# Four small edits around the turn between two images: where sums steps, a row copy, a table load and spilled rows are placed

## The chip, the cores and the metric

The kernel runs on one core of one Trainium2 chip. The metric is the time of one execution on the device in microseconds (us), lower is better. The runs of one kernel mostly lie within 0.2 to 0.5% of each other (no_logs: 1.0%), so a single difference below some 8 us means little; the tables give the medians of several runs and ratios with 95% intervals. All runs told here were in the fast state.

PE is TensorE's matrix array, PEld its weight load, DVE VectorE, ACT ScalarE, POOL GpSimd and SPq the queue from which SyncE starts DMA transfers. L333 means line 333 of that kernel's source; line numbers shift by a few between kernels.

## The reference, cut to what matters

Eight images of 256 channels and 96 x 96 pixels pass through two layers with residuals.

```python
# x: (8, 256, 96, 96) float32
x = x + L0(group_norm(x))   # q, k, v = three 1x1 convolutions, each fft2; q, k normalised;
                            # attention of 32 x 32 per head over frequencies; abs(ifft2); 1x1 convolution
x = x + L1(group_norm(x))   # q = softplus(Wq x + bq), k = softplus(Wk x + bk), v = Wv x + bv;
                            # linear attention: (q . k v) / (q . sum k)
```

## The kernel before

The kernel works through the images in turn. Five stages matter here. The *sums* of an image are 37 steps, each with four transposes (`eoT`), one copy by ScalarE, two sums (`eo`) by VectorE or GpSimd and eight product passes (`acc`). They belong to the next image and are woven as fillers between the matmuls of the present one: `yield n` in a stage lets n of those steps run. The *rotation* transposes all rows of an image (`xr`) and multiplies them by a table (`y`). Then come the *images* stage, the *q and k* stage with the key transposes (`kT`) behind it, and the *output* stage (`o`), whose stores write the image out. The *turn* is the time from the output stage's first matmul to the next image's first `xr` transpose; sums steps that are left over run in it.

```python
T0 = 6                                     # tiles T0 .. 11 of an image go by DRAM, already transposed

def pair_sums(b):                          # one step
    ...
    nc.scalar.activation(both, pt, AF.Copy, scale=pw[:, j:j + 1])
    if b and t >= T0:
        n = P - j // 2                     # 128 or 127 partitions
        for c in range(2):
            nc.sync.dma_start(out=turned(c, PR * t, 1 + P * j)[0:n], in_=both[0:n, c])
    ...
    pool = (j if t < T0 else t > NT - 4) if b and i < len(steps) - 5 else None   # which sums GpSimd takes
    ...
    yield

def rotate(b):
    ...
    o = x_col(0)                           # row 0 into the half that the last image is stored from
    nc.gpsimd.tensor_copy(y[:, :, :, 0], x_of(b)[:, :, o:o + W])
    nc.gpsimd.memset(ys[:, :, 0:1], 0.0)
    ...
    pieces = [TR * i for i in (15, 4, 0, 5, 14, 6, 1, 8, 13, 7, 2, 9, 12, 10, 3, 11)]

def layer1(b):
    for s in range(NS):
        ...                                # two q and k matmul groups, DVE relu, ACT Abs and Exp
        yield 0.5
    ...
    yield 2
    ...                                    # softplus: ACT table load and Ln, DVE adds; then kT
```

Of the kernel before, what the change touches and what calls it, by code (L numbers as in the profile page):

```python
# [53 lines left out]
AF = mybir.ActivationFunctionType  # L54
# [6 lines left out]
D = 32  # L61
ROWS = 8
TR = 6
T0 = 6
NZ = 33
NH = 8
GN_EPS = 1e-5
# [5 lines left out]
def two_layer_kernel(ctx: ExitStack, tc: tile.TileContext, x, w1t, b1, w2t, b2, w3, b3, wot, temp,  # L73
# [26 lines left out]
    def x_of(b):  # L100
        return arenas[b % 2]
# [218 lines left out]
        return t.rearrange("p k (h w) -> p k h w", w=W)  # L320

    s0 = {}

    def pair_sums(b):

        st0 = new_stats(f"st0_{b}")
        acc = [acc_tile(f"acc{c}_{b}") for c in range(2)]

        def products(t, np_, first, last):
            for c in range(2):  # L330
                for m in range(KC):
                    mm = nc.tensor.matmul(acc[c][:, m * C:m * C + (KC - m) * P], lhsT=t[0:np_, c, m * P:(m + 1) * P],  # L332
                                          rhs=t[0:np_, c, m * P:C], start=(first and m == 0), stop=(last and c == 1),  # L333
                                          skip_group_check=True)
                    if first and m:
                        tc.keep_in_program_order(mm)

        x = x_of(b)

        w0 = one.tile([P, KC, H + 1], F32, tag="ys", name=f"w0_{b}")  # L340
        nc.gpsimd.memset(w0[:, :, H // 2:H // 2 + 1 + PR * T0], 0.0)

        def sides(t, j):

            o = (NT - 1 - t) * TW + (t == 0) * W + 1 + P * j
            e = (NT - t) * TW - (t == 0) * W - 1 - P * j
            if t or j < 2:
                return [(0, P, x[:, :, o:o + P], x[:, :, e:e - P:-1])]
            m = H // 2
            rows = [x[:, :, x_col(h):x_col(h) + W] for h in (0, H // 2)] + [w0]  # L350
            if j == 2:
                return [(0, 32, x[:, :, o:o + 32], x[:, :, e:e - 32:-1])] + [
                    (32 * i + 32, 32, v[:, :, 1:33], v[:, :, W - 1:W - 33:-1] if i < 2 else w0[:, :, m + 2:m + 34])
                    for i, v in enumerate(rows)]

            return [(32 * i, 32, v[:, :, m:m + 32], v[:, :, m:m - 32:-1]) for i, v in enumerate(rows[0:2])] + [
                (64, 32, w0[:, :, 32:64], None), (64, 16, None, w0[:, :, m + 33:m + 49]), (80, 16, None, w0[:, :, m:m + 16]),
                (96, 32, rows[0][:, :, 0:32], rows[0][:, :, 0:32])]

        back = three.tile([P, TR * (W + 1)], F32, tag="tm", name=f"back_{b}")[:, 0:2 * C].rearrange(  # L360
            "p (i k n) -> p i k n", i=2, k=KC)

        def turn_back(i):

            t, j = steps[i]
            assert (b, t) in loaded
            if j == 0:
                col = x[:, :, (NT - 1 - t) * TW:(NT - t) * TW:W]
                h, o = PR * t, H // 2 + 1 + PR * t
                nc.gpsimd.tensor_copy(w0[:, :, h:h + PR], col[:, :, 0:PR])  # L370
                if t:
                    nc.gpsimd.tensor_copy(w0[:, :, o:o + PR], col[:, :, :PR - 1:-1])
                else:
                    nc.gpsimd.tensor_copy(w0[:, :, o:o + 1], col[:, :, 0:1])
                    nc.gpsimd.tensor_copy(w0[:, :, o + 1:o + PR], col[:, :, 2 * PR - 2:PR - 1:-1])
                    nc.gpsimd.tensor_copy(w0[:, :, o - 1:o], col[:, :, 2 * PR - 1:])
            if j == 0:
                xts.append(ring_tile(f"xt_{b}_{t}_{j}").rearrange("p (j c n) -> p j c n", j=3, c=2))
            ab = sides(t, j)
            ready = len(ab) == 1  # L380

            front = ab[0][2] if ready else xts[-1][:, j % 3, 0].rearrange("p (k n) -> p k n", k=KC)
            for p0, n, *v in ab:
                for c in range(ready, 2):
                    if v[c] is not None:
                        (nc.scalar.copy if b and t < T0 and (ready or not c) else nc.gpsimd.tensor_copy)(
                            (front, back[:, i % 2])[c][:, :, p0:p0 + n], v[c])
            return front, xts[-1][:, j % 3]

        steps = [(t, j) for t in range(NT - 1, -1, -1) for j in range(3)] + [(0, 3)]  # L390
        pending, first = None, True
        xts = []
        ahead = turn_back(0)
        for i, (t, j) in enumerate(steps):
            front, both = ahead
            pt = ps_tile(f"eoT_{b}_{t}_{j}").rearrange("p (c n) -> p c n", c=2)
            for k in range(KC):
                nc.tensor.transpose(pt[:, 0, k * P:(k + 1) * P], front[:, k], ident)
                nc.tensor.transpose(pt[:, 1, k * P:(k + 1) * P], back[:, i % 2, k], ident)  # L399
            nc.scalar.activation(both, pt, AF.Copy, scale=pw[:, j:j + 1])  # L400
            if b and t >= T0:
                n = P - j // 2
                for c in range(2):
                    nc.sync.dma_start(out=turned(c, PR * t, 1 + P * j)[0:n], in_=both[0:n, c])
            eo = sum_slot()[:, :, 0:C]
            if i + 1 < len(steps):
                ahead = turn_back(i + 1)

            pool = (j if t < T0 else t > NT - 4) if b and i < len(steps) - 5 else None
            for c, (op, on_pool) in enumerate(((ALU.add, nc.gpsimd.tensor_add), (ALU.subtract, nc.gpsimd.tensor_sub))):  # L410
                if pool or pool is None and c:
                    on_pool(eo[:, c], both[:, 0], both[:, 1])  # L412
                else:
                    nc.vector.scalar_tensor_tensor(eo[:, c], in0=pt[:, 0], scalar=pw[:, j:j + 1], in1=both[:, 1],  # L414
                                                   op0=ALU.mult, op1=op)
            if pending is not None:
                products(*pending, first, False)
                first = False
            pending = (eo, P)
            if j in (1, 2):  # L420
                stats_chunk(st0, b, 2 * (NT - 1 - t) + j - 1)
            if (t, j) == (0, 1):
                wl = ring_tile(f"wl_{b}").rearrange("p (k o) -> p k o", k=KC)
                for o, v in enumerate((w1t, w2t, w3)):
                    nc.sync.dma_start(out=wl[:, :, o * C:(o + 1) * C], in_=v.rearrange("(k p) o -> p k o", p=P))
            if b and (t, j) == (T0, 2):
                n = H // 2 - PR * T0
                pt = ps_tile(f"w0T_{b}")
                col = xts[-2][:, 0, 0]
                for k in range(KC):  # L430
                    nc.tensor.transpose(pt[0:H + 1 - PR * T0, k * P:(k + 1) * P], w0[:, k, PR * T0:H + 1], ident)
                nc.scalar.copy(col[0:H + 1 - PR * T0], pt[0:H + 1 - PR * T0, 0:C])
                for c in range(2):
                    o = c * (H // 2 + 1)
                    nc.sync.dma_start(out=xtd[c].rearrange("(h w) n -> h w n", w=W)[:, 0], in_=col[o:o + n])
            yield
        s0[b] = channels(st0, f"a{b}"), acc, products, pending, wl
# [158 lines left out]
    def rotate(b):  # L596

        y = image(y_of(b))
        ys = one.tile([P, KC, H + 1], F32, tag="ys", name=f"ys_{b}")
        o = x_col(0)  # L600
        nc.gpsimd.tensor_copy(y[:, :, :, 0], x_of(b)[:, :, o:o + W])
        nc.gpsimd.memset(ys[:, :, 0:1], 0.0)

        def spilled(h):

            return b > 0 and PR * T0 <= h < H - PR * T0 and h != H // 2
# [18 lines left out]
            return tm  # L625


        pieces = [TR * i for i in (15, 4, 0, 5, 14, 6, 1, 8, 13, 7, 2, 9, 12, 10, 3, 11)]
        order = [h + r for h in pieces for r in range(0, TR, 2)]
        xts = {}  # L630

# [38 lines left out]
        for i, h in enumerate(order):  # L670
            if i % (TR // 2) == 0:
                tm = tms.pop(0)
            if i % (TR // 2) == 2 and i > 2 and pieces:
                tms.append(load_r(pieces.pop(0)))
            if not spilled(h):
                xts[i] = xT[:, i % NX]
            step(None if spilled(h) else h, pending.pop(0) if len(pending) == 2 else None, xts[i])
            pending.append((h, xts.pop(i), tm))
            fetch(i + 3)
            yield  # L680
# [110 lines left out]
    def layer1(b):  # L791
# [30 lines left out]
        for s in range(NS):  # L822
            n = slice(s * CH, (s + 1) * CH)
            for c in range(2):
# [7 lines left out]
                                        op0=ALU.add, op1=ALU.max)  # L832
                nc.scalar.activation(ex[:, c, n], ps[:, 0:CH], AF.Abs, bias=bkqs[:, c:c + 1])
                nc.scalar.activation(ex[:, c, n], ex[:, c, n], AF.Exp, scale=-1.0)
            yield 0.5
        zero = own[:, 5 * C:5 * C + 1]
        nc.scalar.activation(zero, ex[:, 1, NS * CH - 1:NS * CH], AF.Copy, scale=0.0)

# [6 lines left out]
            nc.tensor.matmul(pv[:, 0:C], lhsT=nmb[:, k, :], rhs=wvs[:, k, :], start=(k == 0), stop=(k == KC - 1))  # L845
        nc.vector.tensor_add(bvs, bvs, pv[:, 0:C])

        yield 2

        def softplus(c, s):  # L850

# [228 lines left out]
```

## Time and profile before

| quantity | value |
|---|---|
| time, median of 4 runs | 2750.23 us (2745.97 to 2752.4); 2748.91 in the three known at the prediction |
| PE busy in the profiled run | 2682.8 us, 98% |
| turn, seven images | 48.5 to 51.0 us, mean 49.6 |
| q and k stage, to the first `kT` | 26.6 us, of it PE idle 1.57 |
| rotation, to the images stage | 65.6 us |
| spells at half clock, between 60 and 2600 us | three of 3.4 us |

PE is nearly always busy, so only its work and its few waits count. The prediction below shows and reads the lines: the wait for GpSimd's sum at the turn, where the row copy stands in front of that sum and itself waits for the stores, and the wait for ScalarE behind the logarithms. The rows from the turn down come from the starts of the instructions in the trace and from its records of the clock; "clock" is the granted TensorE clock.

### The profile page before, as it was taken

To read this page: it belongs to the slowest core of one execution; us is meant where nothing else is said; L and a number is where in the kernel's file an instruction comes from. 1 tells how busy PE (TensorE), PEld (TensorE's weight loads), DVE (VectorE), ACT (ScalarE), POOL (GpSimd) and SP (SyncE) were. 2 spreads that over 40 slices of the span, in tenths; PEclk is the share of its full clock that TensorE was granted. 3 is DMA by queue.
4 is the path that set the end of the run, shared out by engine and by line. 5 is a ranking of instruction groups with operands and counts; after the bars stand their busy time and mean duration, and the time that the engine had idled before them with its cause. 6 is when DMAs were issued, how large, how long until landed. Compare 5 with 4: busy or idle time off the path is not lost. (4 is left out here: it accounts for less than half of the span.)

```text
span 2744.9 us, 47959 instructions
## 1 busy us (share of the span) xinstructions
PE 2682.8 (98%) x17718; PEld 1934.5 (70%) x17718; DVE 1971.2 (72%) x4246; ACT 1363.4 (50%) x2167; POOL 854.3 (31%) x1284
## 2 busy tenths in 40 slices
PE   8999999999999999999999999999999999999988
PEld 8965678657795677856678567785677856778556
DVE  6678666886668766687676876769767686677766
ACT  3455643556425564255642546435564355644554
POOL 6133340333404424044140441413414134141311
PEclk9999999999999999999999999999999999999997
DMA  5220264202542026320263203631036311262003
GB/s 174 70 68 12 70 219 129 74 10 96 204 110 69 15 93 207 101 69 20 95 208 103 58 26 99 207 101 52 28 99 210 102 46 33 96 217 70 1 7 138
DMA packets 216407, 261.38 MB, mean 95 GB/s; under 512 B 32624, under 2 KB 204272, under 8 KB 216176
## 3 DMA queue, kind: packets, MB, share of 16 engines
q1 hardware_dynamic: 215232, 257.99, 30.1%
q8 instruction: 142, 2.33, 0.4%
q14 instruction: 89, 0.73, 0.1%
q10 hardware_dynamic: 944, 0.34, 0.0%
HBM read 145.75 MB, written 112.51 MB: 94 GB/s over the span
## 5 line engine op out<-in xcount | busy, mean ns | idle before, releaser
L732 PE MATMUL z<-arena,mz 128*128 128x384 f32 (+2 forms) x2400 | 595.0, 476 | 0.0
L744 PE MATMUL po<-e,wo 128*128 128x384 f32 x1536 | 529.7, 486 | 0.2 <-ACT e L779 0.2
L778 POOL TENSOR_TENSOR e<-e 128x768 f32<-128x768 f32 x192 | 348.7, 1816 | 552.0 <-ACT e L777 551.7
L732 PEld LDWEIGHTS z<-arena,mz 128*128 128x128 f32 (+1 forms) x2400 | 325.6, 163 | 241.4 <-issue 42.4
L332 PE MATMUL acc<-xT 128*128 128x256 f32 (+1 forms) x2368 | 451.7, 332 | 28.2 <-POOL xT L412 16.7
L332 PEld LDWEIGHTS acc<-xT 128*128 128x128 f32 x2368 | 385.0, 192 | 72.5 <-POOL xT L412 19.1
L744 PEld LDWEIGHTS po<-e,wo 128*128 128x128 f32 x1536 | 289.4, 190 | 197.7 <-DVE arena L746 1.2
L656 PE MATMUL y<-tm,xT 96*128 96x97 f32 x3040 | 424.1, 268 | 3.6 <-ACT xT L665 2.9
L773 DVE TENSOR_TENSOR e<-z,xT 128x768 f32<-128x768 f32 x384 | 365.8, 953 | 84.9 <-PE z L732 84.8
L656 PEld LDWEIGHTS y<-tm,xT 96*128 96x128 f32 x3040 | 411.9, 192 | 16.5 <-issue 7.4
L286 DVE BATCH_NORM_STATS2 st<-arena 128x6 f32<-128x384 f32 x768 | 409.4, 553 | 13.3 <-DMA arena<-in_x_dram 2.9
L779 ACT ACTIVATE e<-e 128x768 f32<-128x768 f32 x192 | 162.0, 844 | 337.9 <-POOL e L778 336.9
L777 ACT ACTIVATE e<-e 128x1536 f32<-128x1536 f32 x192 | 284.5, 1482 | 90.3 <-DVE e L773 88.8
L400 ACT ACTIVATE xt<-eoT,pw 128x512 f32<-128x512 f32 x296 | 202.9, 688 | 194.7 <-PE eoT L399 180.3
L746 DVE TENSOR_TENSOR arena<-arena,po 128x384 f32<-128x384 f32 x384 | 211.3, 552 | 90.5 <-PE po L744 67.7
L412 POOL TENSOR_TENSOR xT<-xt 128x256 f32<-128x256 f32 x324 | 236.0, 745 | 63.6 <-ACT xt L400 62.9
L665 ACT COPY xT<-xr 96x512 f32<-96x512 f32 (+1 forms) x223 | 127.5, 576 | 249.1 <-PE xr L653 249.1
L653 PE MATMUL xr<-ident,arena 128*96 128x128 f32 x876 | 229.3, 275 | 0.0
L662 DVE COPY arena<-y 128x384 f32<-128x384 f32 (+1 forms) x384 | 208.9, 547 | 1.8 <-issue 1.2
L414 DVE SCALAR_TENSOR_TENSOR xT<-eoT,pw,xt 128x256 f32<-128x256 f32 x268 | 119.4, 478 | 125.2 <-ACT xt L400 124.9
L661 DVE COPY ys<-y 128x4 f32<-128x4 f32 (+1 forms) x384 | 61.9, 161 | 151.8 <-PE y L656 149.0
L981 DVE TENSOR_TENSOR arena<-arena,o 128x384 f32<-128x384 f32 x288 | 142.6, 550 | 37.3 <-PE o L976 37.2
(227 smaller groups left out, 3254.3 us busy)
## 6 DMA issues: line engine op xcount, KB each, us to landing
arena<-in_x_dram SPq DMA_DIRECT2D x184, 384.0 KB
out_dram<-arena SPq DMA_DIRECT2D x184, 384.0 KB
xT<-xtd SPq DMA_DIRECT2D x161, 192.0 KB
tm<-rx SPq DMA_DIRECT2D x108, 218.2 KB
xtd<-xt SPq DMA_DIRECT2D x168, 128.0 KB
xtd<-xt SPq DMA_DIRECT2D x84, 127.0 KB
rx<-tm SPq DMA_DIRECT2D x16, 218.2 KB
tm<-rt SPq DMA_DIRECT2D x16, 216.0 KB
```

What stands on the lines that cost most here:

```text
L286: nc.vector.bn_stats(out=st[:, k, c, :], in_=x_of(b)[:, k, c * CH:(c + 1) * CH])
L332: mm = nc.tensor.matmul(acc[c][:, m * C:m * C + (KC - m) * P], lhsT=t[0:np_, c, m * P:(m + 1) * P], rhs=t[0:np_, c, m * P:C], start=(first ...
L412: on_pool(eo[:, c], both[:, 0], both[:, 1])
L653: nc.tensor.transpose(pt[0:W, r * C + k * P:r * C + (k + 1) * P], x_of(b)[:, k, o:o + W], ident)
L656: nc.tensor.matmul(pu[:, o:o + W + 1], lhsT=gt[0:W, 1 - r if back else r, k * P:(k + 1) * P], rhs=tm[:, g % TR + r, :], start=True, stop=True)
L662: nc.vector.tensor_copy(y[:, :, :, g + r:g + 2], src[:, :, 0:W, r:2] if back else src[:, :, W - 1::-1, r:2])
L732: mm = nc.tensor.matmul(out[:, o:o + n * W], lhsT=columns(mz, k, c, j), rhs=y[:, k, h * W:(h + n) * W], start=(k == 0 and o == 0), stop=(k ...
L744: nc.tensor.matmul(po[:, 0:CH], lhsT=wo[:, k, m * P:(m + 1) * P], rhs=e[:, k, :], start=(k == 0), stop=(k == KC - 1))
L746: nc.vector.tensor_add(x[:, m, n], x[:, m, n], po[:, 0:CH])
L773: nc.vector.tensor_add(e[:, 2 * c:2 * c + 2, :].rearrange("p t (q h) -> p t q h", h=H), pz[:, 0:CH].rearrange("p (q h) -> p q h", h=H).uns ...
L777: nc.scalar.activation(e, e, AF.Square)
L778: nc.gpsimd.tensor_add(e[:, 0:2, :], e[:, 0:2, :], e[:, 2:4, :])
```

## The change

Its intent: spill a seventh tile by DRAM, so that 16 transposes an image go; issue row 0's copy with its rows instead of ahead of the rotation; let whole instead of half sums steps run beside q and k, so that fewer are left at the turn; and hold the logarithms back until one step's copy is out. The rule for which sums GpSimd takes (`i < 13`) was changed with the seventh tile. It was not run alone; what bounds its worth is said further below.

```diff
-T0 = 6
+T0 = 5
+    evicted = {}
...
+            evicted[0] = both
...
-            pool = (j if t < T0 else t > NT - 4) if b and i < len(steps) - 5 else None
+            pool = (j if t < T0 else i < 13) if b and i < len(steps) - 5 else None
...
-        o = x_col(0)
-        nc.gpsimd.tensor_copy(y[:, :, :, 0], x_of(b)[:, :, o:o + W])
-        nc.gpsimd.memset(ys[:, :, 0:1], 0.0)
...
-        pieces = [TR * i for i in (15, 4, 0, 5, 14, 6, 1, 8, 13, 7, 2, 9, 12, 10, 3, 11)]
+        pieces = [TR * i for i in (15, 4, 0, 5, 6, 14, 8, 3, 1, 7, 9, 13, 10, 12, 11, 2)]
...
+            if h == 0:
+                o = x_col(0)
+                nc.gpsimd.tensor_copy(y[:, :, :, 0], x_of(b)[:, :, o:o + W])
+                nc.gpsimd.memset(ys[:, :, 0:1], 0.0)
...
-            yield 0.5
+            yield 1
...
-        yield 2
+        yield 1
+        if b + 1 < B:
+            nc.scalar.activation(zero, evicted[0][:, 0, 0:1], AF.Identity, scale=0.0, bias=zero)
+        yield 1
```

## The prediction

> **What bounds the kernel now.** I read the page, then the timeline of one image, engine by engine, then sums over stretches. The page says that PE is the bound:
>
> ```profile
> span 2744.9 us, 47959 instructions
> PE 2682.8 (98%) x17718; PEld 1934.5 (70%) x17718; DVE 1971.2 (72%) x4246; ACT 1363.4 (50%) x2167; POOL 854.3 (31%) x1284
> ```
>
> So a gain is either PE work taken away or one of the few PE waits. The list of PE's waits has two lines that come back with the images:
>
> ```profile
> PE acc L332 <- POOL xT L412: 16.7, 15, 2.8
> PE acc L332 <- DVE xT L414: 11.2, 8, 1.6
> ```
>
> The timeline shows where they sit. Images 1 to 7 repeat one pattern of about 336 us; I use image 1. The first is at the end of the sums (the turn into the next image), where PE has only sums left:
>
> ```profile
> 410.84 1.47 PE L332 MATMUL acc<-xT 128*128 128x256 f32 x8
> 412.58 0.82 PE L332 MATMUL acc<-xT 128*128 128x256 f32 x4
> 415.29 0.92 PE L332 MATMUL acc<-xT 128*128 128x256 f32 x4 [1.88 <-POOL xT L412]
> 421.46 1.04 PE L653 MATMUL xr<-ident,arena 128*96 128x128 f32 x8
> ...
> 414.12 0.52 POOL L601 COPY arena<-arena 128x192 f32<-128x192 f32 x1 [3.33 <-DMA wl<-in_w1t_dram]
> 414.50 0.73 POOL L412 TENSOR_TENSOR xT<-xt 128x256 f32<-128x256 f32 x1
> ```
>
> L601 is row 0's copy into the arena from which the previous image is still being stored. GpSimd is in order, so it stands 3.33 us before it, the sum L412 stands behind it, and PE waits for the sum. The releaser's name (a weight load) is a guess of the profile: the data that the copy must wait for are the stores. These are a bound of their own:
>
> ```profile
> 369.00:377.00 8.00, 8.00 (x52) 5.39 (x50) 5.82 (x13) 2.54 (x6) 1.72 (x3) 1.00 0.08 27
> 382.20:414.10 31.90, 31.20 (x224) 23.69 (x224) 25.00 (x54) 16.87 (x38) 20.95 (x38) 1.00 1.05 363
> ```
>
> The last two columns are DMA share and GB/s: from 382.2 to the very moment of the copy, 414.1, all DMA engines are full. The output stage's first matmul is at 372.8, so the stores are through 41.3 us after it, whatever PE does.
>
> The second wait is behind the logarithms, when q and k are done:
>
> ```profile
> 318.37 1.28 ACT L857 ACT_TABLE_LOAD   x1
> 319.66 1.12 ACT L857 ACTIVATE spu<-spu,own 128x384 f32<-128x384 f32 x2
> 320.69 1.24 ACT L400 ACTIVATE xt<-eoT,pw 128x512 f32<-128x512 f32 x2
> ...
> 322.29 1.57 PE L332 MATMUL acc<-xT 128*128 128x256 f32 x8 [1.57 <-DVE xT L414]
> ```
>
> ScalarE takes the table and two logarithms first; the step's copy (L400), transposed by 318.9, starts 1.8 us late.
>
> **What the Trainium skill says.** "ScalarE: Activation LUTs", section What ACT_TABLE_LOAD costs, gives about 1283 ns for a load; the trace has 1.28 us here, and five loads an image. "DMA: Bandwidth & Descriptors", section Why a DMA increments its semaphore by 16 and not by 1, says that a transfer of 127 partitions uses one DMA engine. The share of 0.08 from 369 to 377, with the 127-row writes just issued, agrees (one of 16 is 0.06). "TensorE: Matmul & The Clock Gate", section The HAM clock gate, says that PE drops to half rate after an idle window of about 3.4 us. The trace agrees in kind, not in length: after a wait of 2.8 us in image 5's turn the same transposes took
>
> ```profile
> 1763.13 0.42 PE L398 MATMUL eoT<-ident,xt 128*128 128x128 f32 x1
> ```
>
> against 0.27 us in image 1. "Perfetto Trace Analysis", section Identifying the Most-Contended Engine, warns that busy PE is no measure of headroom; so I count PE by starts of following instructions, not by its durations.
>
> **The change part by part.** Unit costs from starts in the timeline: a whole sums step (4 transposes, 8 product passes) is 1.74 us of PE (406.71 to 408.45, again to about 410.2). An image transpose is 0.11 us (8 between 421.46 and 422.34).
>
> *Seven tiles by DRAM.* The orders of both programs differ by 112 image transposes (876 to 764), 16 in each of seven images: 16 x 0.11 = 1.76 us an image, 12.3 in all, off PE. ScalarE loses 28 copies and 21 of its turned-back copies (these go to GpSimd); neither is the bound. DMA gains 28 reads of 192 KB and 42 writes. In the rotation VectorE then has less cover: a row pair costs it 0.16 + 0.55 us (L661, L662) against PE's 0.85 without transposes. From 432 to 437 it is busy 4.89 of 5.00 us now, and the new order of pieces puts six spilled pairs in a row. I leave 0.4 us an image for that: net -1.4.
>
> *Whole steps beside q and k.* Six steps instead of three there, three fewer at the turn. PE is full in both places, so this moves 3 x 1.74 = 5.2 us, and does not save it. The stage from 297.1 to the first kT at 323.7 grows by 5.2.
>
> *Logarithms behind a step's copy.* The 1.57 us wait goes. But the logarithms now start one copy later (two steps stand between the last kq and kT). From durations: the last kq's Abs and Exp, the copy, the load and one logarithm end about 6.0 us after the last kq, VectorE's add 0.55 later, and kT could start at 6.1. That is a new wait of 0 to 0.6; I take 0.3. Stage: +5.2 - 1.57 + 0.3 = +3.9.
>
> *Row 0's copy later.* In the new order of GpSimd the copy has moved behind all sums but one: the last step's second sum is still after it. So the turn does not become free of the stores. PE's three remaining steps would end early: the last transposes about 38.5 us after the output stage's first matmul, the previous products and the first half of the last about 40.5. Then PE waits for the copy at 41.3 (+0.39 to the next start), the sum 0.73, and the last four passes 0.65: image transposes start at about 43.2. Before it was 421.46 - 372.8 = 48.7. The turn gets 5.4 us shorter; of that, 5.2 is the steps that moved. PE's wait there stays about 2 us (before 1.88 in image 1), so cold clocks stay about as likely.
>
> Sum per image: turn -5.4, q and k +3.9, rotation -1.4, so -2.9; seven turns: -20 us. Image 0's own rotation changes only in order. 2748.9 - 20 = 2729.
>
> **Rivals.** (1) *The stores bind nothing, all waits go.* Then each image gains 1.76 + 1.57 + about 2 to 3 at the turn (the wait, its latency and the cold spells), some 6 us: 2748.9 - 42 = 2707. For it: copy and sums were meant to be untangled. Against it: one sum stays behind the copy in GpSimd's order, and the DMA row is at 1.05 until 414.1. (2) *DMA becomes the bound.* Two more 127-row writes an image on one engine, ahead of the stores in the same queue, could start the stores later; with a longer wait PE goes cold, 1.3 us more (image 5: 8.7 us from copy to first image transpose against 7.3). Reads of 192 KB a pair every 0.85 us, with the row tables, ask some 300 GB/s in the runs of spilled pairs. That could cost 2 to 3 us an image: about 2748, the same. For it: the full DMA row. Against it: tile 5 is written at the same place before the output stage as tile 6 was, because the sums run three steps earlier, and the rotation now moves 124 GB/s. (3) *ScalarE becomes the bound beside q and k.* Per step it has 2 x (0.58 + 0.52) + 0.69 = 2.9 us against PE's 2.65 + 1.74 = 4.4: no.
>
> **Range and chances.** The sure part is the 112 transposes (12 us); the two waits trade against each other and can add 30 or eat it all. Predicted 2729, 8 in 10 between 2705 and 2747. Over 2% faster needs 55 us, more than all waits and transposes of rival 1 together: 0.03. Within 2%: 0.96. Slower: 0.01, only by rival 2 in a strong form.
>
> **What would show it.** Right, if the 1.57 us wait is gone from every image, if the stage from first kq to first kT is near 30.5 us, if the row copy still starts 41 to 42 us after the output stage's first matmul with PE waiting about 2 us just behind it, if the first image transpose is near 43, and if the rotation from there to the images stage is near 64 (65.6 now). Wrong, if PE runs through the turn without a wait (rival 1), if the copy moves to 43 or later or PE waits in the rotation for reads from DRAM (rival 2), or if kT waits over 1 us for the logarithms.

## The result, and the profile after

The changed kernel takes 2736.38 us (median of 4 runs, 2730.56 to 2737.94) against 2750.23. The ratio is 0.9948, with a 95% interval of 0.9928 to 0.9967: the same within 2%, and about 14 us better. All ratios here are the mean time of one kernel's fast runs over the mean of the other's of the same rounds, so they are not quite the ratios of the medians quoted.

The page of the profiled run, first lines:

```profile
span 2728.8 us, 47818 instructions
PE 2679.0 (98%) x17606; PEld 1918.7 (70%) x17606; DVE 1955.3 (72%) x4218; ACT 1343.2 (49%) x2125; POOL 883.3 (32%) x1334
```

PE has 112 instructions less, and only 3.8 us less busy time. The list of PE's waits (line waited at, releaser, us in total, times, longest):

```profile
PE acc L333 <- POOL xT L414: 14.4, 14, 2.3
PE kT L884 <- DVE arena L866: 6.2, 8, 3.6
...
PE acc L333 <- DVE xT L416: 0.2, 1, 0.2
```

The wait for VectorE's sum behind the logarithms has shrunk from 11.2 us to 0.2 in all. In its place, `kT` waits 0.37 us an image (the 3.6 is in the last image). The wait for GpSimd's sum at the turn is still there, 14.4 us instead of 16.7. The timeline of the turn of image 1 (start, duration, then the idle time before it and its releaser; first PE, then GpSimd):

```profile
416.04 2.43 PE L333 MATMUL acc<-xT 128*128 128x256 f32 x12
420.13 1.48 PE L333 MATMUL acc<-xT 128*128 128x256 f32 x4 [1.66 <-POOL xT L414]
421.40 1.49 PE L652 MATMUL xr<-ident,arena 128*96 128x128 f32 x6
...
415.07 0.73 POOL L414 TENSOR_TENSOR xT<-xt 128x256 f32<-128x256 f32 x1 [0.51 <-ACT xt L401]
415.73 0.11 POOL L677 MEMSET ys<- 128x2 f32 x1
418.97 0.51 POOL L676 COPY arena<-arena 128x192 f32<-128x192 f32 x1 [3.13 <-DMA wl<-in_w1t_dram]
419.35 0.72 POOL L414 TENSOR_TENSOR xT<-xt 128x256 f32<-128x256 f32 x1
```

The copy L676 waits 3.13 us for the stores, one sum L414 stands behind it, and PE waits for that sum. The output stage's first matmul started at 377.6, so the copy comes 41.4 us after it and the first `xr` 43.8. This is the knot of before, with fewer sums behind the copy.

Behind the last q and k matmul, on ScalarE and then PE:

```profile
662.24 0.69 ACT L401 ACTIVATE xt<-eoT,pw 128x512 f32<-128x512 f32 x1 [0.71 <-PE eoT L400]
662.96 0.29 ACT L854 ACTIVATE own<-xt,own 128x1 f32<-128x1 f32 x1
663.27 1.28 ACT L864 ACT_TABLE_LOAD   x1
664.56 1.12 ACT L864 ACTIVATE spu<-spu,own 128x384 f32<-128x384 f32 x2
...
665.82 0.55 PE L884 MATMUL kT<-ident,arena 128*128 128x128 f32 x3 [0.37 <-DVE arena L866]
```

The step's copy L401 now comes ahead of the table load, as meant.

Stage by stage, from the starts of PE's instructions, mean of images where they differ (us per image):

| stage | before | after | predicted |
|---|---|---|---|
| turn | 49.6 | 43.6 | 43.2 |
| copy, after the output stage's first matmul | 41.6 | 41.5 | 41 to 42 |
| q and k, to the first `kT` | 26.6 | 31.9 | 30.5 |
| rotation | 65.6 | 63.5 to 63.9 in five images, up to 66.5 | 64 |

Over the seven repeated images of the profiled runs the turns give -41.7 us, the q and k stages +37.5, the rotations -10.2, and the rest about -1.7. That is the -16.1 us between the profiled spans of 2744.9 and 2728.8. The profiled run of the changed kernel is the fastest of its four.

So the number came out close to the prediction. Whether the parts did what it said is another matter, and the sum of four edits cannot tell. The experiments take them apart.

### The profile page after: what moved, and what is told of

Its sections match the earlier page's. It is cut to its first block, busy times and chain, and to the rows that moved or that the text cites. A ratio compares the mean times of both kernels' runs of the same rounds, so it can differ in the third digit from the quotient of the medians.

```text
span 2728.8 us, 47818 instructions
## 1 busy us (share of the span) xinstructions
PE 2679.0 (98%) x17606; PEld 1918.7 (70%) x17606; DVE 1955.3 (72%) x4218; ACT 1343.2 (49%) x2125; POOL 883.3 (32%) x1334
## 5 line engine op out<-in xcount | busy, mean ns | idle before, releaser
L333 PE MATMUL acc<-xT 128*128 128x256 f32 (+1 forms) x2368 | 449.6, 330 | 15.3 <-POOL xT L414 14.4
L655 PE MATMUL y<-tm,xT 96*128 96x97 f32 x3040 | 410.9, 268 | 1.9 <-DMA xT<-xtd 1.3
L655 PEld LDWEIGHTS y<-tm,xT 96*128 96x128 f32 x3040 | 401.7, 192 | 13.8 <-issue 8.0
L401 ACT ACTIVATE xt<-eoT,pw 128x512 f32<-128x512 f32 x296 | 203.4, 687 | 164.0 <-PE eoT L400 151.1
L414 POOL TENSOR_TENSOR xT<-xt 128x256 f32<-128x256 f32 x352 | 256.5, 745 | 60.9 <-ACT xt L401 59.8
L664 ACT COPY xT<-xr 96x512 f32<-96x512 f32 (+1 forms) x195 | 111.2, 574 | 277.4 <-PE xr L652 273.5
L652 PE MATMUL xr<-ident,arena 128*96 128x128 f32 x764 | 200.7, 279 | 0.0
L416 DVE SCALAR_TENSOR_TENSOR xT<-eoT,pw,xt 128x256 f32<-128x256 f32 x240 | 107.2, 478 | 82.1 <-ACT xt L401 82.1
L387 POOL COPY back<-arena 128x256 f32<-128x256 f32 (+1 forms) x230 | 89.2, 396 | 237.5 <-PE eoT L400 237.5
```

What stands on the lines that cost most here:

```text
L333: mm = nc.tensor.matmul(acc[c][:, m * C:m * C + (KC - m) * P], lhsT=t[0:np_, c, m * P:(m + 1) * P], rhs=t[0:np_, c, m * P:C], start=(first ...
L414: on_pool(eo[:, c], both[:, 0], both[:, 1])
L655: nc.tensor.matmul(pu[:, o:o + W + 1], lhsT=gt[0:W, 1 - r if back else r, k * P:(k + 1) * P], rhs=tm[:, g % TR + r, :], start=True, stop=True)
```

## The experiments

Twelve kernels ran; all gave correct results. Those of one batch share the runs of the kernel before; batches ran on different chips, so kernels of different batches are compared by their ratios. In the text, "the copy" is row 0's copy on GpSimd.

| run | what | median us | ratio to before | 95% |
|---|---|---|---|---|
| (the change) | | 2736.38 | 0.9948 | 0.9928 to 0.9967 |
| row_front | change, copy back in its old place in the source | 2731.05 | 0.9942 | 0.9924 to 0.996 |
| row_kept | change, copy held behind the sums | 2717.51 | 0.9893 | 0.9877 to 0.9908 |
| row_kept_only | before, copy held behind the sums | 2725.87 | 0.9926 | 0.9913 to 0.9938 |
| split127 | change, 127-row stores in two | 2714.13 | 0.9876 | 0.9861 to 0.9891 |
| logs_only | before, logarithms behind a copy | 2741.43 | 0.9972 | 0.9963 to 0.9981 |
| no_logs | change without that | 2748.07 | 0.9994 | 0.9983 to 1.0005 |
| t0_six | change with six tiles | 2725.22 | 0.9916 | 0.9903 to 0.9929 |
| half_kept_split | change, both repairs, half steps | 2738.07 | 0.9965 | 0.9953 to 0.9977 |
| whole_only | before, whole steps | 2730.87 | 0.9943 | 0.993 to 0.9957 |
| split_kept | change, both repairs | 2712.73 | 0.9875 | 0.9861 to 0.9888 |
| early_steps | both repairs, three steps moved ahead of q and k | 2721.45 | 0.9911 | 0.9897 to 0.9924 |
| t0_six_split | six tiles and the split | 2724.71 | 0.9911 | 0.9894 to 0.9927 |

### row_front: does the move in the source matter?

```diff
 # on the changed kernel
+        o = x_col(0)                        # ahead of the rotation again
+        nc.gpsimd.tensor_copy(y[:, :, :, 0], x_of(b)[:, :, o:o + W])
+        nc.gpsimd.memset(ys[:, :, 0:1], 0.0)
...
-            if h == 0: ...                  # the same three lines
```

> The changed kernel with row 0's copy put back to the front of the rotation in the source. In the built order of GpSimd it then still stands at the same place, behind all sums but the last. Order theory: what counts is the place in the queue, so nothing changes: 2736 us (within 0.2% of the changed kernel), copy 41 to 42 us after the output stage's first matmul, first image transpose at 43.6. Rival (the move in the source is what shortened the turn): the turn goes back towards 48.7, up to 5 us an image, some 2770 us.

The order of GpSimd's instructions did not change at all: the scheduler, which is free to reorder GpSimd here, hoists the copy to the same slot from either place. The time is that of the changed kernel, 0.9942 against 0.9948. The edit named first in the change does nothing. The profiled run had one long spell of half clock (13.7 us at 423), which made the rotation of image 1 71.3 us (64.4 in split127, which has no spell there).

### row_kept and row_kept_only: hold the copy where the source has it

```diff
 # row_kept: on the changed kernel; row_kept_only: on the kernel before, with the copy moved to `if h == 0`
-                nc.gpsimd.tensor_copy(y[:, :, :, 0], x_of(b)[:, :, o:o + W])
+                tc.keep_in_program_order(nc.gpsimd.tensor_copy(y[:, :, :, 0], x_of(b)[:, :, o:o + W]))
```

> The changed kernel with row 0's copy pinned behind all sums in GpSimd's queue. Queue theory: PE's wait of about 2 us at the turn goes, the first image transpose starts about 41.2 us after the output stage's first matmul in place of 43.6, no cold spells: 2.4 us an image, 2736 - 17 = 2719. Rival (the stores bind anyway, because VectorE's writes of y need them too and PSUM then fills): the wait comes back in the rotation and the time stays at 2733 to 2737.

> The kernel before with nothing changed but row 0's copy in its row's step and pinned behind all sums. Queue theory: the turn loses its wait and its latency, first image transpose at about 46.2 in place of 49.6 (mean of seven images), 3.4 us an image: 2750 - 24 = 2726, so better than the whole change. Rival (stores bind): 2745 or more.

Both came out near what was expected. With the whole change, GpSimd's timeline at the turn of image 1 became

```profile
417.36 0.73 POOL L414 TENSOR_TENSOR xT<-xt 128x256 f32<-128x256 f32 x1 [1.21 <-ACT xt L401]
420.09 0.52 POOL L676 COPY arena<-arena 128x192 f32<-128x192 f32 x1 [2.01 <-DMA wl<-in_w_dram]
```

The last sum is through before the copy, which still waits 2 us for the stores, but nobody stands behind it. The turn is 41.4 us in every image, PE has no wait over 0.1 us behind the output stage's last matmul, and no spell of half clock occurs between 60 and 2600 us. Of the rival, that the wait comes back in the rotation, little is seen: the rotations take 64.0 us in the mean, 63.7 in split_kept, and 0.9 us of PE's waits there are for reads from DRAM. On the kernel before, this one edit makes the turn 46.8 us and is worth at least as much as the whole change (0.9926 against 0.9948, intervals that overlap by a little). What the move in the source was meant to do is worth 15 to 20 us once the scheduler is made to do it.

### split127: let the stores leave sooner

```diff
-                    nc.sync.dma_start(out=turned(c, PR * t, 1 + P * j)[0:n], in_=both[0:n, c])
+                    for lo, hi in ((0, n),) if n == P else ((0, 112), (112, n)):
+                        nc.sync.dma_start(out=turned(c, PR * t, 1 + P * j)[lo:hi], in_=both[lo:hi, c])
```

> The changed kernel with each 127-row write to DRAM issued as 112 and 15 rows, so that it is spread over the DMA engines; the copy stays where it is. Store theory: the first store can be issued before 9.5 us after the output stage's first matmul, the stores and so the row copy end 1 to 2 us earlier than 41.5, and the first image transpose follows them: 2736 - 7 to - 14. Rival (the first store waits for the output's own data, or the end is set by bandwidth and not by the start): the copy stays at 41 to 42 and the time at 2736.

This gave more than expected: about 20 us on top of the change. The DMA queue's timeline at the output stage, first of the changed kernel, then of this one (start, time from the first issue of the line to the end of its last, line, transfer):

```profile
380.05 5.64 SPq L437 DMA_DIRECT2D xtd<-xt  x2
385.73 1.43 SPq L139 DMA_DIRECT2D arena<-in_x_dram  x3
387.21 2.80 SPq L1002 DMA_DIRECT2D out_dram<-arena  x4
```

```profile
374.63 1.19 SPq L438 DMA_DIRECT2D xtd<-xt  x2
378.97 1.42 SPq L139 DMA_DIRECT2D arena<-in_x_dram  x3
383.26 2.57 SPq L1003 DMA_DIRECT2D out_dram<-arena  x4
```

L437 (L438 with the split) is not the 127-row write, which is L406, but the pair of 28-row writes of column 0 that comes last in the spill. One of them takes the queue 0.31 us; what fills the 5.64 us is waiting. The waits of the DMA queue say for what, first in the changed kernel and then with the split (us in total, times, longest):

```profile
SPq L437 <- DMA xtd<-xt: 70.8, 14, 5.5
SPq L438 <- DMA xtd<-xt: 4.6, 9, 1.6
```

Each of the pair waits until a spill write issued earlier has landed, 10.1 us an image together, and with the 127-row writes split 0.7. So in the changed kernel the queue hangs behind the spill writes until 385.7, and the first output store follows 9.6 us after the output stage's first matmul. With the split it follows after 5.3. DMA was far from busy in the meantime. The windows of the changed kernel (busy time and count of PE, PEld, DVE, ACT, POOL; then the clock, DMA share and GB/s):

```profile
374.00:382.00 8.00, 8.00 (x51) 5.24 (x49) 5.64 (x12) 2.44 (x5) 1.90 (x3) 1.00 0.09 30
382.50:387.00 4.50, 4.50 (x36) 3.50 (x37) 4.16 (x10) 2.77 (x6) 3.64 (x6) 1.00 0.10 23
387.00:419.00 32.00, 31.29 (x220) 23.34 (x220) 26.23 (x55) 15.85 (x38) 21.62 (x46) 1.00 1.03 361
```

Before the stores leave, the engines stand at a share of 0.09 to 0.10, little more than one of sixteen (0.06); after that they are full until the copy. With the split the stores have begun by then: the stretch from 383.5 to 387 has 0.82 and 293 GB/s. The copy comes at 39.4 us in the mean instead of 41.5. The turn falls to 41.4 us (42.7 in image 1), there is no cold spell, and the rotations take 63.5 us (64.4 in image 1).

### logs_only and no_logs: the logarithms alone, and the change without them

```diff
 # logs_only: on the kernel before; no_logs takes the same lines out of the changed kernel
+            evicted[0] = both
...
-        yield 2
+        yield 1
+        if b + 1 < B:
+            nc.scalar.activation(zero, evicted[0][:, 0, 0:1], AF.Identity, scale=0.0, bias=zero)
+        yield 1
```

> The kernel before with only the logarithms put behind a step's copy. Theory of the prediction: the wait of 1.57 us goes, kT then waits 0 to 0.6 us for the logarithms; the stage from the first kq to the first kT shrinks from 26.6 to about 25.4, 7 x 1.2 = 8 us: ratio to before 0.997. Rival (the later table load only moves the wait to kT): ratio 1.000.

> The changed kernel without the logarithms' extra wait. Theory: the wait of some 1.5 us for VectorE's or GpSimd's sum comes back in each of seven images and the wait before kT goes, so the stage grows from 31.9 by 1.0 to 1.5: 7 to 10 us above the changed kernel, ratio to before 0.9975. Rival (with whole steps the logarithms no longer stand in a step's way): no change, 0.9945.

Alone, the edit takes the q and k stage from 26.6 to 25.5 us: 1.57 us of wait go and 0.57 of `kT` wait come. That is 7.7 us (2748.3 x 0.0028), as expected. Taken out of the changed kernel, the stage grew by the 1.2 us an image that was expected (33.1), but the time grew by more than expected (0.9994 instead of 0.9975), and its 22 runs spread over 27 us: the fastest had a mean clock of 0.993, the slowest of 0.983. The windows of the rotation of image 2 in the profiled run (clock 0.985), with the wait ahead of it, show what happened there:

```profile
757.00:760.00 3.00, 0.00 (x0) 0.00 (x0) 0.15 (x1) 0.00 (x0) 0.95 (x2) 0.91 0.99 273
760.00:777.50 17.50, 17.28 (x85) 15.41 (x86) 6.51 (x24) 4.24 (x8) 0.51 (x3) 0.53 0.26 67
777.50:795.00 17.50, 17.50 (x128) 15.21 (x127) 11.19 (x31) 3.89 (x9) 0.00 (x0) 1.00 0.36 99
```

PE stands still from 757 to 760, and then works 17 us at a clock of 0.53: 85 instructions in a stretch where the next one of equal length has 128. That rotation took 70.6 us, and another with a spell of 13.7 us took 70.0.

### whole_only: whole steps and nothing else

```diff
 # on the kernel before
-            yield 0.5
+            yield 1
```

> The kernel before with one edit: whole sums steps beside the q and k matmuls. The row copy keeps its old place in the source. Theory (it is the whole steps, not the move of the copy in the source, that changed which sums stand ahead of the copy on GpSimd): the copy comes after all but one of GpSimd's sums, as in the changed kernel, the stores start earlier because three steps of the sums lie before the output stage, and the first image transpose falls from 49.6 us after the output stage's first matmul to about 42 us. The q and k stage takes about 33 us (it keeps the wait of 1.6 us for the table load), the rotation stays at 65.6 us. Sum per image: -7.5 +6.5, about -1 us, ratio 0.996 to 0.999. Rival (the place in the source decides): the turn stays at about 49 us, only the q and k stage grows, and the ratio is above 1.01.

The order is as the theory said, though the copy's place in the source is that of before (GpSimd, turn of image 1):

```profile
415.76 0.74 POOL L412 TENSOR_TENSOR xT<-xt 128x256 f32<-128x256 f32 x1 [0.50 <-ACT xt L400]
416.43 0.11 POOL L602 MEMSET ys<- 128x2 f32 x1
418.77 0.51 POOL L601 COPY arena<-arena 128x192 f32<-128x192 f32 x1 [2.23 <-DMA out_dram<-arena]
419.15 0.72 POOL L412 TENSOR_TENSOR xT<-xt 128x256 f32<-128x256 f32 x1
```

One sum stands behind the copy, as in the changed kernel. Here the releaser is named as what it is, the stores. The turn is 41.4 us (42.2 in image 1), q and k 33.0, as expected. The time is better than expected, 0.9943 instead of 0.996 to 0.999, because the turn fell by 8.1 us and not by 7.5, the stages from the first `kT` to the output got 0.3 us shorter, and some 4 us of the profiled run went outside the seven repeats. **One edited number gives as much as the whole change.** It does so because the sums are three steps ahead: the last spill writes leave earlier, and the first store comes 5.1 us after the output stage's first matmul instead of 9.5.

### t0_six and t0_six_split: what is the seventh tile worth?

```diff
 # t0_six: on the changed kernel; t0_six_split: with the split of split127 as well
-T0 = 5
+T0 = 6
...
+        pieces = ...                        # the order of before
```

> The changed kernel with six tiles by DRAM, and the old order of pieces. The rotation grows by the 16 transposes, from 63.5 to about 65.6. Store theory: the last tile's 127-row writes are through three steps sooner, so the stores start and end sooner, the row copy is at about 39 and the first image transpose at 41.4 in place of 43.6: the two nearly cancel, ratio to before 0.9945. Rival (the writes of tile 5 do not delay the stores): copy still at 41 to 42, 7 x 2.1 = 15 us above the changed kernel, ratio 1.000.

> The changed kernel with six tiles by DRAM and the old order of pieces, as in the run with six tiles, and now with its 127-partition stores split into 112 and 15 as well. Theory (the split pays because with seven tiles the one-engine stores hold back the output stores; with six they are issued three steps earlier and already leave in time): first output store near 5 us, first image transpose 41.2 to 42 us, rotation 65.6, ratio 0.990 to 0.9925, as with six tiles unsplit (0.9916); then the seventh tile with split stores (0.9876) is worth about 10 us. Rival (the split saves some 20 us in any kernel, by what it takes off one DMA engine): ratio 0.985 or less.

Without the seventh tile the change is faster, 0.9916 against 0.9948: 9 us by the ratios, of which the intervals just touch, and 6 between the profiled runs. The theory had the two equal, so its time missed. Its mechanism held: the rotation is 65.6 us again, the first store comes after 5.1 us instead of 9.6, the copy after 39.4, and the turn is 41.2 to 42.5. The split adds nothing there (0.9911), as the theory said: with six tiles the spill writes are through in time anyway. Together:

| ratio to before | stores of 127 rows whole | split |
|---|---|---|
| six tiles | 0.9916 | 0.9911 |
| seven tiles | 0.9948 | 0.9876 |

As written, the seventh tile costs about 9 us; with its writes split it gains about 10. The stages of the profiled runs say where. With whole writes the rotations give 10.2 us (the cold spells of images 1 and 2 and waits for reads take part of what the transposes save), the turns cost 14.1 and the stages between the first `kT` and the output 2.0: +6. With split writes the rotations give 13.9, the turns cost 0.7 and those stages 1.8: -12. The prediction's "sure part" was not sure.

### half_kept_split, split_kept and early_steps: combinations

```diff
 # split_kept: the changed kernel with the edits of row_kept and split127
 # half_kept_split: split_kept, and
-            yield 1
+            yield 0.5
 # early_steps: half_kept_split, and in the images stage
-            yield 1.5
+            yield 3
```

> Seven tiles, row copy pinned behind the sums, 127-row writes spread, logarithms behind a copy, but half steps beside q and k as before. Switch theory: alternating q, k and sums every step costs PE about 0.2 us a time, so with nothing holding PE at the turn the three steps are cheaper there: q and k stage 25.5 to 26, first image transpose at 46.8, rotation 63.5; against 49.6, 26.6 and 65.6 before that is 5.9 us an image, 41 us: ratio 0.985. Rival (the stores, which start later since tile 5 is written later, hold VectorE's writes of y): PE waits in the rotation, ratio 0.988 or more.

> The changed kernel with both repairs: the copy held in its place behind the sums, and every store of 127 partitions split into 112 and 15. If each repair removes the same 2 us of TensorE's wait at the turn, they don't add: first image transpose 41.4 us after the output stage's first matmul in every image, rotation 63.5 us, no spell of half clock, ratio 0.987, as for the split alone (0.9876). If the two act on different waits, they add, and the ratio is 0.980 or less.

> The kernel with both repairs, half steps beside q and k again, and three of the sums steps moved to the end of the stage that forms the image ahead. Theory (switching between q/k and sums matmuls is what made the q and k stage longer than the sums moved there): q and k stage 25.5 us, the images stage 5.2 us longer, no longer turn than with both repairs, so 0.6 to 1 us less per image, ratio 0.002 below the kernel with both repairs. Rival (VectorE, ScalarE and GpSimd have no room there, as in the stage of the key transposes with half steps and six tiles): a new wait of over 1 us per image in the images stage, ratio no better or worse than with both repairs.

**split_kept** came out as its theory had it. The two repairs remove the same wait and don't add: 0.9875 against 0.9876 for the split alone. The turn is 41.4 us in every image. This kernel and split127 are the fastest of all, 34 us below the kernel before.

**half_kept_split** missed by some 30 us. The q and k stage was 25.5 us as expected and the rotation 63.5, but the stage of the key transposes grew from 39.1 to 43.1. The list of PE's waits shows three new lines there, one wait an image each:

```profile
PE kx L874 <- ACT xT L897: 7.5, 7, 1.6
PE xT L894 <- ACT xt L897: 7.3, 7, 1.3
PE xT L894 <- DVE xT L899: 6.5, 7, 0.9
```

These waits of 21.3 us together account for most of the miss. Which of ScalarE's and VectorE's other work in this stage made those copies late I did not take apart. The seventh tile's own steps are not in it: it holds the steps numbered 11 to 15, as in the kernel before, and that tile's are 18 to 20. The changed rule moves the sums of steps 11 and 12 to GpSimd; no run tests whether that matters.

**early_steps** missed too. I had blamed the cost of whole steps on switching between q or k and sums. The q and k stage fell by 6.45 us, but the images stage grew by 7.8: 1.7 are waits, of which 1.27 are one new wait,

```profile
PE eoT L400 <- POOL back L387: 10.7, 9, 1.3
```

for GpSimd's turned-back copy, and 6.1 are the three steps. So three steps cost nearly the same in the images stage (6.1) as beside q and k (6.45). It isn't q and k that makes them dear. The PE timeline beside q and k in the changed kernel shows what does:

```profile
649.65 0.33 PE L399 MATMUL eoT<-ident,arena 128*128 128x128 f32 x1
...
650.15 1.47 PE L333 MATMUL acc<-xT 128*128 128x256 f32 x8
651.55 2.79 PE L832 MATMUL kq<-arena,wkq 128*32 128x384 f32 x32
654.27 0.33 PE L399 MATMUL eoT<-ident,arena 128*128 128x128 f32 x1
```

A step between other work takes 1.90 us from its first transpose to the next matmul (649.65 to 651.55), against 1.74 where steps follow each other. The first transpose has 0.164 us to the next start instead of 0.109, and the last pass 0.204 instead of 0.11. The q and k matmul ahead of it loses another 0.14. Three such steps are 3 x (1.90 + 0.14) = 6.1; the other 0.3 is a wait in the first of them, whose sums come late.

## Why the prediction was right or wrong, point by point

**The time.** 2729 was predicted, 2736 measured, within the range of 2705 to 2747 and within 2%. The mechanism at the turn was as told: the copy at the time of the stores (41.5 us), one sum behind it, PE waiting 1.1 to 2.3 us. Rival 1 fell. The sign of rival 2 in the rotation, PE waiting for reads from DRAM, came only faintly, with 1.3 us in four waits.

**The term that was mis-sized.** "PE is full in both places, so this moves 3 x 1.74 = 5.2 us, and does not save it." The three steps cost 6.45 us beside q and k (25.5 in logs_only, 31.9 in the changed kernel), because 1.74 had been read where steps stand together. So the stage grew by 5.3 instead of 3.9. The logarithms' part of it was right within 0.2: -1.1 against -1.57 + 0.3.

**The rotation.** 2.1 us were gained instead of 1.4 where neither a spell nor a wait for reads fell. The 0.4 that I left for VectorE did not come. And I overlooked a wait of 0.4 us an image for ScalarE's copy, which stands in the kernel before and in t0_six, and not in the changed kernel:

```profile
PE y L656 <- ACT xT L665: 2.9, 7, 0.4
```

So 1.76 for the transposes and 0.4 for the wait make the 2.1. Image 1 gains 1 us less even without a spell (64.4 to 64.7 us in split127, split_kept and row_kept), and spells of half clock ate more in images 1 and 2.

**What the total hid.** Part by part, in us over the whole run, worked out from the ratios times 2749 where a run has the part alone:

| part | predicted | measured |
|---|---|---|
| whole steps with the copy's new order | 7 x (5.2 - 5.4), about -1 | -16 (whole_only) |
| logarithms | 7 x (-1.57 + 0.3), about -9 | -8 (logs_only) |
| seven tiles, with their order of pieces | 7 x -1.4, about -10 | +9 (the change against t0_six) |
| sum | -20 | -14 to -15 |

The first two measured alone add up to -23.4, and t0_six, which has both (and the change's rule for which sums GpSimd takes), is at -23.1. So these parts add, the rule is worth next to nothing there, and the +9 belongs to the seventh tile with its order of pieces. Intervals of 0.1 to 0.2% are some 3 to 5 us to either side, so the 9 is a rough figure. Two steps of the working failed, and their errors cancelled:

- I compared the store's start with that of the kernel before only: "tile 5 is written at the same place before the output stage as tile 6 was". That is true (9.6 and 9.5 us), and it hid both effects. Whole steps by themselves bring the stores forward by 4.4 us; the seventh tile's 127-row writes push them back by 4.5. My rival 2 had this mechanism, and I set it aside with that sentence. Its size, 2 to 3 us an image, was about right: the turn is 2.0 us longer than in t0_six.
- "In the new order of GpSimd the copy has moved behind all sums but one" is right. I took the move in the source for its cause. row_front and whole_only show that the move does nothing, and that the whole steps do it.

**Clock.** "Cold clocks stay about as likely" holds in kind: two spells instead of three. I had put a spell at 1.3 us. In row_front and no_logs a spell of 13.7 to 17.1 us cost a rotation about 7.

The traces also show which waits bring a spell; I had overlooked it. In each trace the spells start on a grid of 3.413 us: those of the changed kernel, at 420.34 and 758.26, are 99 steps apart. Four windows of this grid at its turns (length, busy time of PE, PEld, DVE, ACT, POOL; clock, DMA share, GB/s):

```profile
416.92:420.34 3.42, 1.72 (x9) 1.26 (x8) 1.86 (x3) 0.05 (x1) 1.31 (x4) 1.00 0.92 285
754.84:758.26 3.42, 1.28 (x6) 0.96 (x6) 1.44 (x3) 0.00 (x0) 1.38 (x4) 1.00 1.02 310
1758.40:1761.81 3.41, 2.29 (x13) 1.75 (x11) 2.09 (x4) 0.69 (x1) 0.00 (x0) 1.00 1.04 310
1761.81:1765.22 3.41, 2.17 (x18) 2.12 (x19) 0.63 (x4) 1.22 (x3) 1.45 (x4) 1.00 0.82 192
```

In images 1 and 2 the wait (1.66 and 2.10 us) lies in one window, PE is busy for about half of it or less, and the next window runs at half clock. In image 5 the wait is longer, 2.32 us, but an edge of the grid cuts it in two, and no spell follows. Between 70 and 2600 us of all fourteen traces, 14 of the 15 spells follow a window with PE busy for at most 1.72 us; four other windows, of 1.59 to 1.71 us, were not followed by one, and of the windows above 1.72 only one was, in row_kept_only. So, as far as the trace's modelled ends of PE's instructions tell, it is the length of the wait together with its place on the grid that decides, and the place changes from image to image.

What stays open: why some spells last four or five windows, what started the one in row_kept_only, and what makes the copies late in half_kept_split.

## What to carry to other kernels

When several edits meet at one hand-over, run each alone: here a gain of 16 and a loss of 9 looked like two modest gains. Find out what starts the transfer on which a hand-over waits; here stores held up behind the badly shaped small writes of one tile cost as much as the 16 transposes an image that this tile saved, or more. Moving an instruction in the source moves nothing if a scheduler orders it: look at the order of the engine's instructions, and pin it if it must move.

## What the Trainium skill lacked or had wrong

- "DMA: Bandwidth & Descriptors", section Why a DMA increments its semaphore by 16 and not by 1: its rule (127 partitions on one engine, 112 on sixteen, 15 on fifteen) agrees with the runs as far as they show it (a share of 0.09 to 0.10 behind the whole writes, one of sixteen being 0.06), and the split chosen by it brought the first store from 9.6 to 5.3 us. What the page lacks is what such a write costs those that wait for it: here two small writes behind it stood in the queue for 10.1 us an image, and the output stores behind them.
- "TensorE: Matmul & The Clock Gate", section The HAM clock gate, asks for an idle window of about 3.4 us before half rate. Here a window that PE was busy for half was enough (1.72 of 3.41 us, after a wait of 1.66), in 14 of 15 spells. The spell in row_kept_only, in the middle of a rotation with PE busy throughout, follows no such window.
- The same section has full rate back after about 3.4 us of work. Twelve of the 15 spells lasted that, but three 13.7 and 17.1 us, with PE busy in all of them but for the end of the wait at their start. The page's section PE-mode transpose says that transposes don't count as busy in the same way. That doesn't explain them: two of the windows in no_logs at half clock, from 766.3 to 773.1 us, hold 0.00 and 0.26 us of image transposes among 18 matmuls each.
- No page that I read has the cost of changing between kinds of matmul: here 0.16 us for each sums step that stands alone (1.90 instead of 1.74 us), and about 0.14 us more at the end of the q and k group ahead of it.
